# Layer 3 of a four-layer graph network: seven half-products with W1 in the place of eight, and one norm for both halves

## The chip, the cores and the metric

The kernel runs on one core of one Trainium2 chip. The metric is the device time of that core in microseconds (us): the time before is the median of three runs, 4798.12 us (4796.85 to 4800.23). The profile comes from one further, profiled execution.

## The reference

Sixteen graphs of 1024 nodes with 256 features pass through four layers, each of the form x = x + layer(relu(layernorm(x)), adj). All arithmetic is in float32. The change lies in layer 3 alone, which computes, per graph:

```
h   = relu(layernorm(x))                          # 1024 x 256
agg = epsilon * h + adjacency @ h                 # 1024 x 256
h   = agg @ W1 + b1                               # 1024 x 1024
h   = silu(h * rsqrt(mean(h*h, over its 1024 columns) + 1e-6) * rms_weight)
out = h @ W2 + b2                                 # 1024 x 256
x   = x + out
```

## The kernel before, in words

Layers 0 and 1, then layer 2 and then layer 3 follow one another; layer 3 starts near 3400 us of the span and takes the rest. It goes through the 16 graphs ("batches" b) one after the other. All of it works on transposed data: features lie on the 128 partitions, nodes along the free axis. N = 1024 nodes are cut into two halves of NH = 512[...]. D = 256 makes DC = 2 blocks of 128 features, H = 1024 makes HC = 8 blocks.

For each batch the functions inside `layer_3` do this:

- `load(b)` (L1105) issues the DMAs on SP's queue: x, the layer's other input hn, and the transposed adjacency in two halves `at[b][0]`, `at[b][1]`. Tiles come from pools with a fixed number of buffers per name; a load starts when a buffer of that name is free. hn lies in the pool `shared` under the name "hb", two buffers, which at the start hold x and hn of batch 0.
- `prepare(b)` (L1120) adds hn to x, takes mean and variance, and writes h = relu(layernorm(x)); VectorE does the adds and statistics, GpSimd the power -1/2 (L83) and the adds of epsilon on the diagonal of the adjacency (L1124), ScalarE the relus (L1143), and GpSimd at last adds b2 to x (L1146).
- `sums(b)` (L1148) is the product with the adjacency, in four parts (half of N, block of D), each eight matmuls of 512 columns into a bank "pa" (L1155), copied to the tile ag by ScalarE or VectorE (L1158, L1160).
- `inner(ag, n0, between)` (L1163) is the product with W1 for one half of N: for each of the 8 blocks k of H two matmuls (L1170) into a bank "ph" (two banks), then ScalarE squares it (L1173), VectorE copies it to hh with b1 (L1174), and GpSimd adds the squares up in ss (L1176). `between` names steps of the other half's norm to be put behind block k.
- `norm` (L1181) gives `mean` (four matmuls with a column of ones, L1188, and the power), `spread` (four transposes that put the result in a bank "pr", L1194) and `apply` (multiply by it on VectorE, L1199, and silu on ScalarE, L1200).
- `outer` (L1203) is the product with W2: for each of four tiles of 128 nodes eight matmuls of 256 columns into a bank "po" (L1208) and an add onto x (L1211). After the second half x goes out by a DMA on GpSimd's queue (L1245).

The order of the work is set by the loop at the end: inner of half 0; inner of half 1 with the mean and spread of half 0 in between; the four `apply` of half 0; part 0 of the next batch's `sums`; mean of half 1; part 1; spread of half 1; outer of half 0 with `apply` of half 1 between its tiles; part 2; `prepare(b + 2)`; part 3; outer of half 1. From this written order the framework makes each engine's queue: written order is the priority, and an instruction that would have to wait by its reckoning can be passed by a later one that is ready. `tc.issue_after(last)` keeps prepare's VectorE instructions behind the last add of the first `outer`. On the chip each engine runs its queue in order.

Of the kernel before, what the change touches and what calls it, by code (L numbers as in the profile page):

```python
# [9 lines left out]
F32 = mybir.dt.float32  # L10
AF = mybir.ActivationFunctionType
ALU = mybir.AluOpType
# [4 lines left out]
P = 128  # L17
B, N, D, H = 16, 1024, 256, 1024
NT = N // P
DC = D // P  # L20
HC = H // P
# [9 lines left out]
RMS_EPS = 1e-6  # L31
# [9 lines left out]
def gnn_stack(ctx: ExitStack, tc: tile.TileContext, a: dict, out: bass.AP):  # L41
    nc = tc.nc
# [3 lines left out]
    ident = const.tile([P, P], F32, name="ident")  # L46
    make_identity(nc, ident)
    ones = const.tile([P, P], F32, name="ones")
# [993 lines left out]

    def early_3(shared, pool, x, hn, at, h):


        eps = pool.tile([P, 1], F32, name="eps")
        nc.sync.dma_start(eps, bcast_row(a["epsilon"], 1))
        x[0] = shared.tile([P, NT, D], F32, name="hb")  # L1050
        nc.sync.dma_start(x[0], rows(x2_d[0]))
        at[0] = [shared.tile([P, NT, 512], F32, name="bxt")]
        for t in range(0, NT, 2):
            nc.sync.dma_start(at[0][0][:, t : t + 2], rows(a["adjT"][0])[:, t : t + 2, :512])
        hn[0] = shared.tile([P, NT, D], F32, name="hb")
        nc.sync.dma_start(hn[0][:, : NT - 2], rows(hn_d[0])[:, : NT - 2])
        nc.sync.dma_start(hn[0][:, NT - 2], hs_d[NT - 2][0][:P])
        eye = pool.tile([P, P], F32, name="eye")
        yield eye

        n = NT - 1
        nc.vector.tensor_scalar(eye, ident, eps, None, op0=ALU.mult)
        mv = pool.tile([P, n, 2], F32, name="mv")
        for t in range(n):
            nc.vector.tensor_add(x[0][:, t], x[0][:, t], hn[0][:, t])
            st = pool.tile([P, 6], F32, name="st", bufs=4)
            nc.vector.bn_stats(st, x[0][:, t])
            nc.vector.bn_aggr(mv[:, t], st)
            if t % 3 == 2:
                yield  # L1070
        rs = inv_sqrt(pool, mv[:, :, 1], LN_EPS, [P, n], "rs")
        for t in range(NT // 2):
            own = at[0][0][:, t, t * P : (t + 1) * P]
            nc.gpsimd.tensor_tensor(own, own, eye, ALU.add)
        yield
        h[0] = hn[0]
        shift = pool.tile([P, n], F32, name="shift")
        nc.vector.scalar_tensor_tensor(shift, mv[:, :, 0], -1.0, rs, op0=ALU.mult, op1=ALU.mult)
        for t in range(n):
            nc.scalar.activation(h[0][:, t], x[0][:, t], AF.Relu, bias=shift[:, t : t + 1], scale=rs[:, t : t + 1])  # L1080
        yield

    def layer_3(shared, x, hn, at, h, eye):
        with ExitStack() as st:
            wp = st.enter_context(tc.tile_pool(name="w3", bufs=1))
# [15 lines left out]
            nc.sync.dma_start(b2, bcast_row(a["b2"], D))  # L1101

            NH = 512

            def load(b):  # L1105
                if b:
# [11 lines left out]
                    at[b].append(half)  # L1118

            def prepare(b):  # L1120
                def diagonal(half):
                    for t in range(half * NT // 2, (half + 1) * NT // 2):
                        own = at[b][half][:, t, t * P % NH : t * P % NH + P]
                        nc.gpsimd.tensor_tensor(own, own, eye, ALU.add)  # L1124
                part = slice(0 if b else NT - 1, NT)
                if b:
                    diagonal(0)
                    h[b] = big.tile([P, NT, D], F32, name="h", bufs=2)
                tiles = range(NT)[part]
                mv = small.tile([P, NT, 2], F32, name="mv")  # L1130
                for t in tiles[::2]:
# [10 lines left out]
                for k, t in enumerate(tiles):  # L1142
                    nc.scalar.activation(h[b][:, t], x[b][:, t], AF.Relu, bias=shift[:, k : k + 1], scale=rs[:, k : k + 1])  # L1143
                diagonal(1)
                for t in range(NT):
                    nc.gpsimd.tensor_tensor(x[b][:, t], x[b][:, t], b2, ALU.add)  # L1146

            def sums(b):  # L1148

                ag = big.tile([P, DC, N], F32, name="ag")  # L1150

                def part(n0, c):
                    pa = psum.tile([P, NH], F32, name="pa")
                    for mt in range(NT):
                        nc.tensor.matmul(pa, h[b][:, mt, c * P : (c + 1) * P], at[b][n0 // NH][:, mt],  # L1155
                                         start=mt == 0, stop=mt == NT - 1)
                    if c == 0:
                        nc.scalar.copy(ag[:, c, n0 : n0 + NH], pa)  # L1158
                    else:
                        nc.vector.tensor_copy(ag[:, c, n0 : n0 + NH], pa)  # L1160
                return ag, [lambda n0=n0, c=c: part(n0, c) for n0 in range(0, N, NH) for c in range(DC)]

            def inner(ag, n0, between):  # L1163

                hh = big.tile([P, HC, NH], F32, name="hh")
                ss = small.tile([P, NH], F32, name="ss")
                for k in range(HC):
                    ph = psum.tile([P, NH], F32, name="ph")
                    for c in range(DC):
                        nc.tensor.matmul(ph, w1[:, c, k * P : (k + 1) * P], ag[:, c, n0 : n0 + NH],  # L1170
                                         start=c == 0, stop=c == DC - 1)
                    sq = ss if k == 0 else small.tile([P, NH], F32, name="sq")
                    nc.scalar.activation(sq, ph, AF.Square, bias=b1[:, k : k + 1])  # L1173
                    nc.vector.tensor_scalar(hh[:, k], ph, b1[:, k : k + 1], None, op0=ALU.add)  # L1174
                    if k:
                        nc.gpsimd.tensor_tensor(ss, ss, sq, ALU.add)  # L1176
                    if k in between:
                        between[k]()
                return hh, ss

            def norm(hh, ss):  # L1181

                got = {}

                def mean():
                    pq = psum.tile([P, NH // P], F32, name="pq", bufs=1)
                    for n in range(NH // P):
                        nc.tensor.matmul(pq[:, n : n + 1], ss[:, n * P : (n + 1) * P], ones[:, 0:1], start=True, stop=True)  # L1188
                    got["rms"] = inv_sqrt(small, pq, RMS_EPS, [P, NH // P], "rms", mul=1.0 / H)

                def spread():
                    pr = psum.tile([P, NH], F32, name="pr", bufs=1)
                    for n in range(NH // P):
                        nc.tensor.transpose(pr[:, n * P : (n + 1) * P], got["rms"][:, n : n + 1].to_broadcast([P, P]), ident)  # L1194
                    got["pr"] = pr

                def apply(quarter):
                    for k in (2 * quarter, 2 * quarter + 1):
                        nc.vector.tensor_mul(hh[:, k], hh[:, k], got["pr"])  # L1199
                        nc.scalar.activation(hh[:, k], hh[:, k], AF.Silu, scale=rw[:, k : k + 1])  # L1200
                return mean, spread, apply

            def outer(b, hh, n0, apply=None):  # L1203
                for k in range(NH // P):
                    t = n0 // P + k
                    po = psum.tile([P, D], F32, name="po")
                    for c in range(HC):
                        nc.tensor.matmul(po, hh[:, c, k * P : (k + 1) * P], w2[:, c], start=c == 0, stop=c == HC - 1)  # L1208
                    if apply:
                        apply(k)  # L1210
                    last = nc.vector.tensor_add(x[b][:, t], x[b][:, t], po)  # L1211
                return last.ins

            load(0)
            prepare(0)
            load(1)
            ag, parts = sums(0)
            for part in parts:
                part()
            prepare(1)  # L1220
            for b in range(B):
                if b + 2 < B:
                    load(b + 2)
                hh0, ss0 = inner(ag, 0, {})
                mean0, spread0, apply0 = norm(hh0, ss0)
                hh1, ss1 = inner(ag, NH, {1: mean0, 4: spread0})
                mean1, spread1, apply1 = norm(hh1, ss1)
                parts = [lambda: None] * 4
                if b + 1 < B:
                    ag, parts = sums(b + 1)  # L1230
                for k in range(4):
                    apply0(k)
                parts[0]()
                mean1()
                parts[1]()
                spread1()
                last = outer(b, hh0, 0, apply1)
                parts[2]()
                if b + 2 < B:

                    with tc.issue_after(last):
                        prepare(b + 2)
                parts[3]()
                outer(b, hh1, NH)
                nc.gpsimd.dma_start(rows(out[b]), x[b])  # L1245

    layers_0_1()
# [51 lines left out]
```

## Time and profile before

| what | value |
|---|---|
| median of three runs | 4798.12 us |
| the profiled execution's own time | 4804.16 us |
| its span, first to last instruction | 4802.5 us |
| mean granted TensorE clock | 0.979 |
| PE (matmul) busy | 4482.4 us, 93% |
| PEld (weight load) busy | 3004.1 us, 63% |
| DVE (VectorE) busy | 2250.0 us, 47% |
| POOL (GpSimd) busy | 1561.7 us, 33% |
| ACT (ScalarE) busy | 1238.4 us, 26% |

The groups of layer 3's window that matter for the change, each with its line, count, and the mean duration of one instruction:

| line, engine | what | count | mean ns |
|---|---|---|---|
| L1170 PE | matmul with W1, 512 columns | 1024 | 607 |
| L1208 PE | matmul with W2, 256 columns | 2048 | 379 |
| L1155 PE | matmul with the adjacency, 512 columns (two groups: 512 and 448 of the records) | 960 | 593 |
| L1173 ACT | square, from PSUM | 224 | 686 |
| L1174 DVE | copy with b1, from PSUM | 256 | 749 |
| L1176 POOL | add to ss | 224 | 1271 |
| L1199 DVE | multiply, one operand in PSUM | 256 | 680 |
| L1200 ACT | silu, from SBUF | 256 | 712 |
| L1158 ACT | copy from PSUM | 32 | 577 |
| L1160 DVE | copy from PSUM | 32 | 692 |
| L1133 DVE | add of two SBUF tiles, 512 columns | 60 | 692 |

How to read it: matmuls overlap in the pipeline, so that the mean duration of one is longer than the distance from one to the next. "Idle before, releaser" in a row is the time for which the engine stood still before an instruction, and what ended it. The chain is the work that ended last, followed back from its end. Where a row of the timeline has a count (x8), the time is that of the whole stretch.

### The profile page before, as it was taken

To read this page: it belongs to the slowest core of one execution; us is meant where nothing else is said; L and a number is where in the kernel's file an instruction comes from. 1 tells how busy PE (TensorE), PEld (TensorE's weight loads), DVE (VectorE), ACT (ScalarE), POOL (GpSimd) and SP (SyncE) were. 2 spreads that over 40 slices of the span, in tenths; PEclk is the share of its full clock that TensorE was granted. 3 is DMA by queue.
4 is the path that set the end of the run, shared out by engine and by line. 5 is a ranking of instruction groups with operands and counts; after the bars stand their busy time and mean duration, and the time that the engine had idled before them with its cause. 6 is when DMAs were issued, how large, how long until landed. Compare 5 with 4: busy or idle time off the path is not lost. (4 is left out here: it accounts for less than half of the span.)

```text
span 4802.5 us, 52444 instructions
## 1 busy us (share of the span) xinstructions
PE 4482.4 (93%) x18199; PEld 3004.1 (63%) x18199; DVE 2250.0 (47%) x6292; ACT 1238.4 (26%) x2629; POOL 1561.7 (33%) x1938
## 2 busy tenths in 40 slices
PE   8998899999997989999999999998899999999999
PEld 4444455555555777777777778777455565655656
DVE  6667845456543444444444444455333334334342
ACT  1111112212111222222332322233222323223232
POOL 3223233344323323232223232323333334333331
PEclk9999999999998999999999999999899999999999
DMA  4333235554546444544353445431422222222200
GB/s 152 115 105 105 80 80 185 198 179 155 183 130 197 127 150 126 157 133 152 111 158 117 141 142 176 129 124 39 136 88 97 79 88 79 88 97 79 79 27 18
DMA packets 530979, 576.63 MB, mean 120 GB/s; under 512 B 42544, under 2 KB 439472, under 8 KB 528304
## 3 DMA queue, kind: packets, MB, share of 16 engines
q1 hardware_dynamic: 499536, 460.27, 30.8%
q0 software_dynamic: 31040, 111.44, 6.7%
q8 instruction: 198, 3.24, 0.3%
q14 instruction: 205, 1.68, 0.1%
HBM read 469.65 MB, written 116.65 MB: 122 GB/s over the span
## 5 line engine op out<-in xcount | busy, mean ns | idle before, releaser
L295 PE MATMUL pa<-at,h 128*128 128x512 f32 x1088 | 502.2, 615 | 32.9 <-DVE ag L300 32.9
L1170 PE MATMUL ph<-ag,w 128*128 128x512 f32 x1024 | 467.3, 607 | 8.4 <-DVE hh L1174 8.3
L1208 PE MATMUL po<-w,hh 128*128 128x256 f32 x2048 | 447.7, 379 | 0.0
L623 PE MATMUL pf<-hb,ab 128*128 128x256 f32 x1568 | 419.1, 385 | 29.4 <-DVE bxt L773 16.2
L1208 PEld LDWEIGHTS po<-w,hh 128*128 128x128 f32 x2048 | 387.8, 190 | 59.3 <-issue 7.9
L295 PE MATMUL pa<-at,q 128*128 128x512 f32 x960 | 424.0, 595 | 0.0
L295 PEld LDWEIGHTS pa<-at,h 128*128 128x128 f32 x1088 | 211.6, 197 | 281.3 <-issue 235.5
L735 PE MATMUL pf<-hs,wx 128*128 128x256 f32 x1536 | 348.9, 381 | 18.7 <-POOL hs L726 16.1
L1170 PEld LDWEIGHTS ph<-ag,w 128*128 128x128 f32 x1024 | 179.8, 190 | 259.5 <-issue 146.5
L1176 POOL TENSOR_TENSOR ss<-ss,sq 128x512 f32<-128x512 f32 x224 | 284.6, 1271 | 149.9 <-ACT sq L1173 149.4
L735 PEld LDWEIGHTS pf<-hs,wx 128*128 128x128 f32 x1536 | 290.4, 191 | 61.4 <-POOL hs L726 17.9
L623 PEld LDWEIGHTS pf<-hb,ab 128*128 128x128 f32 x1568 | 277.7, 192 | 69.3 <-DVE bxt L773 23.5
L295 PEld LDWEIGHTS pa<-at,q 128*128 128x128 f32 x960 | 178.2, 190 | 215.9 <-issue 212.6
L1174 DVE TENSOR_SCALAR hh<-ph,b 128x512 f32<-128x512 f32 x256 | 191.6, 749 | 219.1 <-ACT sq L1173 171.0
L770 PE MATMUL pf<-bd,h 128*128 128x384 f32 (+5 forms) x768 | 213.9, 372 | 49.1 <-DVE bxt L773 26.5
L1022 POOL DMA_INDIRECT hs_d<-h,table x128 | 129.6, 1012 | 368.7 <-ACT gates L743 184.5
L1155 PE MATMUL pa<-at,h 128*128 128x512 f32 x512 | 225.8, 593 | 0.0
L83 POOL TENSOR_TENSOR rs<-rs_v,mhalf 128x8 f32<-128x8 f32 (+1 forms) x65 | 106.9, 1644 | 346.0 <-DVE rs_v L79 332.5
L1173 ACT ACTIVATE sq<-ph,b 128x512 f32<-128x512 f32 x224 | 153.6, 686 | 223.2 <-PE ph L1170 218.1
L773 DVE TENSOR_TENSOR bxt<-bxt,pf 128x384 f32<-128x384 f32 (+5 forms) x384 | 141.3, 384 | 144.3 <-PE pf L770 141.8
L1200 ACT ACTIVATE hh<-hh,rw 128x512 f32<-128x512 f32 x256 | 168.5, 712 | 142.4 <-DVE hh L1199 140.4
L1155 PE MATMUL pa<-bxt,h 128*128 128x512 f32 x448 | 197.4, 593 | 0.0
(261 smaller groups left out, 7271.7 us busy)
## 6 DMA issues: line engine op xcount, KB each, us to landing
at<-in_adjT SPq DMA_DIRECT2D x64, 1024.0 KB, 7.2
ab<-in_adj SPq DMA_DIRECT2D x128, 512.0 KB, 4.1
bxt<-in_adjT SPq DMA_DIRECT2D x64, 512.0 KB, 5.8
at<-in_adjT SPq DMA_DIRECT2D x64, 512.0 KB, 5.8
ad<-in_adj SPq DMA_DIRECT2D x128, 128.0 KB, 5.7
x_d<-x POOLq DMA_DIRECT2D x16, 1024.0 KB, 5.4
he_d<-h POOLq DMA_DIRECT2D x16, 1024.0 KB, 9.2
heT_d<-hT POOLq DMA_DIRECT2D x16, 1024.0 KB, 4.2
```

Source lines behind the costliest of these rows:

```text
L295: nc.tensor.matmul(pa, h[:, mt, c * P : (c + 1) * P], at[n0 // 512][:, mt], start=mt == 0, stop=mt == NT - 1)
L623: nc.tensor.matmul(pb, ab[:, jts[k]], hb[:, jts[k]], start=k == 0, stop=k == len(jts) - 1)
L735: nc.tensor.matmul(pg[:, e], wx[:, c, q * D + e * P : q * D + (e + 1) * P], self.hs[:, c], start=c == 0, stop=c == DC - 1)
L770: nc.tensor.matmul(pf, h[:, g, c * P : (c + 1) * P], bd[:, g, b4 : b4 + 4, S : S + far], start=True, stop=True)
L773: return lambda: nc.vector.tensor_add(to, to, pf)
L1155: nc.tensor.matmul(pa, h[b][:, mt, c * P : (c + 1) * P], at[b][n0 // NH][:, mt], start=mt == 0, stop=mt == NT - 1)
L1170: nc.tensor.matmul(ph, w1[:, c, k * P : (k + 1) * P], ag[:, c, n0 : n0 + NH], start=c == 0, stop=c == DC - 1)
L1173: nc.scalar.activation(sq, ph, AF.Square, bias=b1[:, k : k + 1])
L1174: nc.vector.tensor_scalar(hh[:, k], ph, b1[:, k : k + 1], None, op0=ALU.add)
L1176: nc.gpsimd.tensor_tensor(ss, ss, sq, ALU.add)
L1200: nc.scalar.activation(hh[:, k], hh[:, k], AF.Silu, scale=rw[:, k : k + 1])
L1208: nc.tensor.matmul(po, hh[:, c, k * P : (k + 1) * P], w2[:, c], start=c == 0, stop=c == HC - 1)
```

## The change

In layer 3 the product of agg with W1 is seen as a 2 x 2 block product: D in two halves (c), H in two halves (p), N in two halves. The eight half-products become seven, after Strassen (in Winograd's form). Three combinations of W1's quarters (`ws`) and one that takes the place of a quarter (a21) are made once per kernel by four adds on GpSimd. Per batch four combinations of the sums (`tt`) are made by VectorE. `inner` handles both halves of N at once: for each of four k it does seven products, each one matmul of 512 columns; ScalarE copies the first to SBUF (p1), VectorE adds the next two up (u2, u3), and four results are formed by VectorE with b1 (`result`), then squared by ScalarE from SBUF and added up by GpSimd. The seventh product is accumulated onto the bank of the fourth after VectorE has read that.

With it change the buffers and the order. `mean` and `spread` treat both halves at once and stand after part 0 and part 1 of the next batch's sums; parts 2 and 3 follow, then the first `outer`, then `prepare(b + 2)`, then the second `outer`. ag has one buffer (before: two). The banks "pa" and "ph" become five banks "ph"; "pq", "pr" and "po" become three banks "po". h of a batch is written over hn in its buffer, and x of batch 0 moves to a buffer of its own when b2 is added. All four parts of the sums are copied by ScalarE.

```diff
@@ layer_3, once
+            HH = HC // 2
+            ws = wp.tile([P, 3, HH * P], F32, name="ws")
+            a11, a12, a21, a22 = (w1[:, c, p * HH * P : (p + 1) * HH * P] for p in range(2) for c in range(2))
+            nc.gpsimd.tensor_tensor(ws[:, 0], a21, a22, ALU.add)
+            nc.gpsimd.tensor_tensor(ws[:, 1], ws[:, 0], a11, ALU.subtract)
+            nc.gpsimd.tensor_tensor(a21, a11, a21, ALU.subtract)
+            nc.gpsimd.tensor_tensor(ws[:, 2], a12, ws[:, 1], ALU.subtract)
@@ prepare
-                    h[b] = big.tile([P, NT, D], F32, name="h", bufs=2)
+                    h[b] = hn[b]
...
+                to = x[b] if b else big.tile([P, NT, D], F32, name="x", bufs=3)
                 for t in range(NT):
-                    nc.gpsimd.tensor_tensor(x[b][:, t], x[b][:, t], b2, ALU.add)
+                    nc.gpsimd.tensor_tensor(to[:, t], x[b][:, t], b2, ALU.add)
+                x[b] = to
@@ sums
-                ag = big.tile([P, DC, N], F32, name="ag")
+                ag = big.tile([P, DC, N], F32, name="ag", bufs=1)
+                tt = big.tile([P, 4, NH], F32, name="tt", bufs=1)
+                b21 = []
...
-                    pa = psum.tile([P, NH], F32, name="pa")
+                    pa = psum.tile([P, NH], F32, name="ph", bufs=5)
...
-                    if c == 0:
-                        nc.scalar.copy(ag[:, c, n0 : n0 + NH], pa)
-                    else:
-                        nc.vector.tensor_copy(ag[:, c, n0 : n0 + NH], pa)
+                    nc.scalar.copy(ag[:, c, n0 : n0 + NH], pa)
+                    if (n0, c) == (0, 1):
+                        b21.append(pa)
+                    if (n0, c) == (NH, 0):
+                        nc.vector.tensor_sub(tt[:, 0], pa, ag[:, 0, :NH])
+                    if (n0, c) == (NH, 1):
+                        nc.vector.tensor_sub(tt[:, 1], pa, tt[:, 0])
+                        nc.vector.tensor_sub(tt[:, 2], pa, ag[:, 0, NH:])
+                        nc.vector.tensor_sub(tt[:, 3], b21[0], tt[:, 1])
@@ inner, for both halves of N
-                for k in range(HC):
-                    ph = psum.tile([P, NH], F32, name="ph")
-                    for c in range(DC):
-                        nc.tensor.matmul(ph, w1[:, c, k * P : (k + 1) * P], ag[:, c, n0 : n0 + NH],
-                                         start=c == 0, stop=c == DC - 1)
-                    sq = ss if k == 0 else small.tile([P, NH], F32, name="sq")
-                    nc.scalar.activation(sq, ph, AF.Square, bias=b1[:, k : k + 1])
-                    nc.vector.tensor_scalar(hh[:, k], ph, b1[:, k : k + 1], None, op0=ALU.add)
-                    if k:
-                        nc.gpsimd.tensor_tensor(ss, ss, sq, ALU.add)
-                    if k in between:
-                        between[k]()
+                hh = [big.tile([P, HC, NH], F32, name=f"hh{q}", bufs=1) for q in range(2)]
+                ss = [small.tile([P, NH], F32, name=f"ss{q}", bufs=1) for q in range(2)]
+                begun = [False, False]
+
+                def product(lhsT, rhs, onto=None):
+                    ph = onto if onto is not None else psum.tile([P, NH], F32, name="ph", bufs=5)
+                    nc.tensor.matmul(ph, lhsT, rhs, start=onto is None, stop=True, skip_group_check=onto is not None)
+                    return ph
+
+                def result(k, q, ph, u):
+                    nc.vector.scalar_tensor_tensor(hh[q][:, k], ph, b1[:, k : k + 1], u, op0=ALU.add, op1=ALU.add)
+                    sq = small.tile([P, NH], F32, name="sq") if begun[q] else ss[q]
+                    nc.scalar.activation(sq, hh[q][:, k], AF.Square)
+                    if begun[q]:
+                        nc.gpsimd.tensor_tensor(ss[q], ss[q], sq, ALU.add)
+                    begun[q] = True
+
+                for k in range(HH):
+                    mine = slice(k * P, (k + 1) * P)
+                    p1, u2, u3 = (small.tile([P, NH], F32, name=name) for name in ("p1", "u2", "u3"))
+                    ph = product(a11[:, mine], ag[:, 0, :NH])
+                    nc.scalar.copy(p1, ph)
+                    ph = product(ws[:, 1, mine], tt[:, 1])
+                    nc.vector.tensor_add(u2, ph, p1)
+                    ph = product(a21[:, mine], tt[:, 2])
+                    nc.vector.tensor_add(u3, ph, u2)
+                    p5 = product(ws[:, 0, mine], tt[:, 0])
+                    result(HH + k, 1, p5, u3)
+                    result(HH + k, 0, product(a22[:, mine], tt[:, 3]), u3)
+                    result(k, 0, product(a12[:, mine], ag[:, 1, :NH]), p1)
+                    result(k, 1, product(ws[:, 2, mine], ag[:, 1, NH:], p5), u2)
@@ norm: mean and spread for both halves, apply inside spread
+                    pq = psum.tile([P, N // P], F32, name="po", bufs=3)
...
+                    for q in range(2):
+                        pr = psum.tile([P, NH], F32, name="po", bufs=3)
...
+                        for k in range(HC):
+                            nc.vector.tensor_mul(hh[q][:, k], hh[q][:, k], pr)
+                            nc.scalar.activation(hh[q][:, k], hh[q][:, k], AF.Silu, scale=rw[:, k : k + 1])
@@ the loop over batches
-                hh0, ss0 = inner(ag, 0, {})
-                mean0, spread0, apply0 = norm(hh0, ss0)
-                hh1, ss1 = inner(ag, NH, {1: mean0, 4: spread0})
-                mean1, spread1, apply1 = norm(hh1, ss1)
+                hh, ss = inner(*ags)
+                mean, spread = norm(hh, ss)
...
-                for k in range(4):
-                    apply0(k)
                 parts[0]()
-                mean1()
+                mean()
                 parts[1]()
-                spread1()
-                last = outer(b, hh0, 0, apply1)
+                spread()
                 parts[2]()
+                parts[3]()
+                last = outer(b, hh, 0)
                 if b + 2 < B:

                     with tc.issue_after(last):
                         prepare(b + 2)
-                parts[3]()
-                outer(b, hh1, NH)
+                outer(b, hh, 1)
```

## The prediction

> **What bounds the kernel now.** I read the table of engines first (PE busy 93% of the span), then a window over one batch of layer 3 in mid-run, then the chain in that window, then the weight loads, which show stalls that a pipelined matmul row hides, and last the first batch. The window is 86.10 us, from one batch's first product with W1 to the next batch's:
>
> ```profile
> core 0: us, PE busy (x) PEld busy (x) DVE busy (x) ACT busy (x) POOL busy (x), PEclk, DMA share, GB/s
> 4476.70:4494.56 17.86, 17.86 (x41) 6.94 (x40) 7.18 (x10) 6.18 (x9) 9.79 (x8) 1.00 0.35 118
> 4494.56:4507.23 12.67, 12.67 (x39) 6.07 (x38) 8.13 (x14) 7.17 (x11) 8.64 (x7) 1.00 0.00 1
> 4507.23:4521.44 14.21, 14.21 (x44) 6.98 (x43) 2.24 (x5) 3.21 (x5) 2.30 (x2) 1.00 0.00 0
> 4521.44:4562.80 41.36, 41.36 (x163) 30.40 (x161) 14.76 (x39) 9.64 (x17) 10.69 (x17) 1.00 0.29 102
> ```
>
> PE is busy throughout at full clock, and no other engine reaches 70% of the first two rows, the stage of `inner`. The chain in that window is PE alone:
>
> ```profile
> by line: PE ph L1170 35.5%; PE po L1208 34.5%; PE pa L1155 27.6%; PE pq L1188 1.6%; PE pr L1194 0.9%
> 4476.86 17.87 PE ph L1170 x40
> 4494.73 0.79 PE pq L1188 x8
> 4495.51 5.43 PE ph L1170 x12
> 4501.38 3.44 PE ph L1170 x8
> 4505.68 1.72 PE ph L1170 x4
> ```
>
> Every float32 matmul of the source is two records (1024 on L1170 for 512 calls). The eight in 3.44 us give 0.429 us a record, 0.858 us a call; the group's mean of 607 ns overlaps its neighbours and is not the price. At 0.429 the 64 records of L1170 need 27.4 us; they took 17.87+5.43+3.44+1.72 = 28.46. The missing 1.0 us shows in the weight loads, where each second k waits for VectorE to empty one of two PSUM banks (0.68 us against the ordinary 0.24 "issue"):
>
> ```profile
> 4479.27 0.19 PEld L1170 LDWEIGHTS ph<-ag,w 128*128 128x128 f32 x1 [0.24 <-issue]
> 4480.14 0.30 PEld L1170 LDWEIGHTS ph<-ag,w 128*128 128x128 f32 x2 [0.68 <-DVE hh L1174]
> ```
>
> So in this layer a matmul removed is time removed, as long as nothing slower takes the stage.
>
> **Removed.** For the output blocks k and k+4 and both halves of N, eight calls become seven: 28 calls of the same shape per batch in place of 32, 4 x 0.858 = 3.4 us. The two-bank stall goes too (five banks now): 1.0 us. The means and transposes keep their counts (8 and 8 calls a batch; 2.5 us before, 2.5 after), `sums` and `outer` keep theirs (27.5 and 27.6 us). A clean batch is then 24.0 + 2.5 + 27.5 + 27.6 = 81.7 us, 4.4 us less.
>
> **Added in the stage, per k of four, beside 7 x 0.858 = 6.0 us of PE:**
> - VectorE: two adds of PSUM and SBUF (nearest row L1199, 680 ns) and four scalar_tensor_tensor. No row has that one at 512 columns: at 256, L397 takes 481 ns against 420 for an add (L1211), so 680+61, about 0.74; L1174 at 512 columns takes 749. I take 0.75. Sum 2 x 0.69 + 4 x 0.75 = 4.4 us, under 6.0.
> - ScalarE: a copy (L1158, 577 ns) and four squares, now from SBUF (L1200 reads SBUF: 712; L1173 reads PSUM: 686): 0.59 + 4 x 0.7 = 3.4 us.
> - GpSimd: four adds into ss as before, 1.27 us each: 5.1 us (14 adds, 17.8 us a batch, under 24.0).
>
> Whether GpSimd stretches when VectorE works harder: the two rows disagree by kind of operand. In the first batch an add of two SBUF tiles beside an ss add slowed both (the two L1133 took 2.36 us where they take 1.29, the ss add 1.55); an L1199 (one operand in PSUM) beside ss adds shows 675 to 689 throughout. All six new operations have one operand in PSUM, so L1199 is near: no stretch. The upper bound is 1.55.
>
> One rule speaks against leaving this add where it is. The row is L1176's 1271 ns against 692 for L1133 on VectorE. The Trainium skill, page GPSIMD Engine Reference, section 4.1 Engine selection, sends elementwise adds of two inputs to VectorE since GpSimd is about twice as slow. By the rule the 14 adds would be 9.7 us on VectorE, whose stage would be 17.5 + 9.7 = 27.2 us against PE's 24.0, and a batch would gain 28.46 - 27.2, just over 1 us. By the rows, 17.8 us on GpSimd lie under 24.0. I go by the rows.
>
> **The new wait.** Product 7 accumulates onto product 4's bank, so it waits for VectorE's first result. Behind it in PE's queue stand the next k's products; who waits for them is the copy p1. From the start of a k: product 1 readable at 0.86 + 0.2 (in the window, first matmul 4476.86, first square 4478.61: two calls plus 0.04 to 0.2), p1 to 1.65, product 2 readable 1.92, u2 to 2.6, product 3 at 2.77, u3 to 3.5, product 4 at 3.63, result to 4.4. Product 7's weights load at 4.9: slack 0.5 us, no stall.
>
> Over several k there is a loop: ScalarE may square the fourth result before it copies p1 of the next k, and a square needs one of two sq tiles, freed by GpSimd. If it does, the loop from one first result to the next is square 0.72, two GpSimd adds 2.6, square 0.74, copy 0.59, u2 0.72, u3 0.69, result 0.75 = 6.8 us, over 6.0. It has no hold in k = 0, whose first two squares go to ss directly; worked forward it costs PE 0.4 us in k = 2 and 0.8 in k = 3, 1.2 us a batch. If the copy goes first, the loop loses a square and an add, and at 4.8 to 5.5 us is under 6.0: 0. The trace before shows ScalarE's later-written silus slipped between squares that wait, so I take 0 and keep 1.2.
>
> **The joint norm.** From the last product: result 0.95, square 0.7, add 1.3, about 3 us, 4.5 with a backlog. The first part of `sums`, 8 calls, 6.9 us, stands between and hides it. The power (1.02 for four columns, 1.65 for eight) and two handoffs lie under the second part's 6.9. After the transposes VectorE's 16 multiplies (0.64 each in a row, 10.3) and ScalarE's 16 silus (0.66, 10.6) run about 12 us under parts three and four, 13.7 us; the first half is ready after 6.5. The four subtractions and ScalarE's copies of the sums (2.8 us, 2.3) follow, and `outer` gives them 27 us. All at 0. Without this cover each exposed us costs 15.
>
> **Prepare moves behind the fourth part.** Before, from its first VectorE add at 4449.69 to shift at 4457.38 is 7.7 us, the relus end about 4462.1, GpSimd's b2 adds at 4464.1: 14.4 us. It began 27.5 us ahead of the next `inner`; now 13.8. All it issues counts: VectorE's 22 operations stand ahead of `outer`'s adds of the second half (three PSUM banks give PE 10.3 us, need 7.7: 0), the relus ahead of the next p1, the b2 and diagonal adds ahead of the output's DMA and of the first ss add, which comes 5 us into `inner`. 0, at most 1 us a batch. Loads on SP's queue: h in hn's buffer frees it only after the sums, which still leaves half a batch or more.
>
> **First and last batch, and the weights.** Batch 0 lasted 96.8 us (3432.51 to 3529.32), 10.7 over a clean one: hn of batch 1 waited for a buffer until 3432.74, and its prepare fell into `inner`:
>
> ```profile
> 3438.53 2.36 DVE L1133 TENSOR_TENSOR x<-x,hb 128x512 f32<-128x512 f32 x2 [0.92 <-DMA hb<-hn_d]
> 3446.08 5.46 PE L1170 MATMUL ph<-ag,w 128*128 128x512 f32 x8 [6.43 <-DVE hh L1174]
> ```
>
> Now x of batch 0 leaves its buffer when the b2 adds end (3421.7), so hn loads some 10 us earlier; its relus and b2 adds still reach into `inner`. I take half, 5 us back (0 to 10). The last batch has no sums to hide the norm: result, square, add, means, power, transposes, multiply, silu expose about 8 us, and the first tile goes at the silus' pace, 5.6 for 3.45: its chain is some 61.5 to 64 us for 60.0 now. I take +3, so no saving there. The four weight sums on GpSimd (5.1 us) can delay the power at 3411.15 if W1 lands first: +1 (0 to 5).
>
> Sum against the profiled execution (4802.5 span, 4804.16 its own time): 14 batches x -4.4 = -62; batch 0 -4.4 - 5; last +3; weights +1: -67.4, so 4736.8. It ran 6.0 over the median of the runs: **4731**.
>
> **Rivals.**
> - ScalarE takes the square before the copy: 15 x 1.2 = 18 more, 4749. For it: that is the order written. Against: a square that waits lets others past.
> - The norm is not covered (means wait for ss by 2 us or more a batch): 4731 + 15 x 2 to 3, about 4770. Against: 6.9 us of cover for 4.5.
> - Slower: GpSimd becomes the bound in that loop, at ss. It decides when the loss reaches the 4.4 us gained: about 2.2 loop turns a batch bite, so a loop of 8.0 us, adds of 1.9 us. At 2.2 us the loop is 8.7, 5.9 us a batch are lost and 1.5 net, and with the first and last batch the kernel stands near 4820. Against: 1.55 is the slowest ss add in the trace.
> - The matmuls removed were not on the path: 4798. Against: the chain.
>
> **Chances.** The forecast 0.52 (its own range 4718 to 4742), the loop in the written order 0.28, the norm exposed 0.09, no change 0.04, slower 0.07. About 0.2% (9.6 us) is what a measurement here can tell from no change. Faster 0.89, same 0.04, slower 0.07. Range: low, batch 0 gives all 10 back and weights and tail cost nothing, 4722, less 4 for overlap of the means; high, the loop's case with batch 0 giving nothing, the weights at 5 and prepare at 0.7 a batch: 4769.
>
> **What would show it.** A batch of 81.7 us, 56 records of the products in 24.0, their weight loads idle 0.24 throughout; waits of PE on the second result line near zero. A p1 copy that starts after the fourth square, with squares waiting on ss, shows the loop; PE waiting on ss at the means, the norm. The forecast is wrong if ss adds pass 1.5 us, or if VectorE's new operations pass 0.9 us.

## The result, and the profile after

The changed kernel takes 4758.98 us (median of four runs, 4754.82 to 4763.29) where the kernel before takes 4799.17 beside it (4796.85 to 4805.13): a ratio of 0.9914, 95% interval 0.9897 to 0.9932. The forecast was 4731 in a range of 4718 to 4769; the time lies in the range, but 28 us behind the forecast, and nearer to the rival of the written order, 4749. It lies in the range because that was drawn wide enough for this rival; the forecast itself had put the rival's cost at nothing.

The profiled execution has a span of 4753.1 us, 49.4 less than before. Not all of that is the change's: layer 3's first matmul starts at 3392.10 where it started at 3401.66, and over the runs of this study it started between 3386 and 3402 us, in no order that follows the edits. So I compare layer 3 alone, from its first matmul to the end of the span: 1400.8 us before, 1361.0 after, 39.8 less.

One batch after, in two windows (columns as before): the seven products, then the rest up to the next batch's first product. They sum to 83.08 us, 86.10 before.

```profile
core 0: us, PE busy (x) PEld busy (x) DVE busy (x) ACT busy (x) POOL busy (x), PEclk, DMA share, GB/s
4428.55:4453.88 25.33, 24.57 (x58) 10.48 (x57) 16.42 (x24) 10.47 (x18) 14.62 (x14) 1.00 0.26 83
4453.88:4511.63 57.75, 57.75 (x217) 39.09 (x216) 21.94 (x52) 17.81 (x31) 16.06 (x21) 1.00 0.26 91
```

The second row is what was forecast (2.5 + 27.5 + 27.6 = 57.6 us): the joint norm, the subtractions and the moved prepare cost PE nothing. The first is not: 25.3 us for 24.0, and PE is idle for 0.8 of it. The chain over this batch (in the window of both rows), which was PE alone before, now leaves PE for a fifth of the time:

```profile
by line: PE po L1251 33.5%; PE ph L1176 33.2%; PE ph L1197 8.6%; POOL ss L1205 6.1%; ACT sq L1203 3.8%; DVE hh L1201 3.7%; DVE u L1216 2.5%; DVE u L1214 2.5%; PE po L1231 2.0%; ACT p L1212 1.7%; issue 1.3%; PE po L1239 1.1%; DVEq L1216 0.1%
```

Its pieces in order of time (start, us, what), from one first result of a k to the next:

```profile
4438.34 0.76 DVE hh L1201
...
4439.18 0.64 ACT sq L1203
...
4439.95 2.52 POOL ss L1205 x2
...
4442.50 0.63 ACT sq L1203
4443.13 0.48 ACT p L1212
...
4443.64 0.70 DVE u L1214
...
4444.43 0.70 DVE u L1216
...
4445.23 0.76 DVE hh L1201
```

This is the loop of the prediction, operation by operation: result, square, two adds on GpSimd, the square that waited for a buffer, the copy behind it, u2, u3, the next result. From 4438.34 to 4445.23 it takes 6.89 us; 6.8 was worked out. The weight loads show where it meets PE, at product 7 of k = 2 and k = 3 (idle 0.98 and 1.44 us for the ordinary 0.24):

```profile
4446.03 0.30 PEld L1197 LDWEIGHTS ph<-ag,ws 128*128 128x128 f32 x2 [0.98 <-DVE hh L1201]
4452.91 0.30 PEld L1197 LDWEIGHTS ph<-ag,ws 128*128 128x128 f32 x2 [1.44 <-DVE hh L1201]
```

Product 7 of k = 2 starts 0.3 us late and that of k = 3 another 0.8; with 0.1 us for each restart that is 1.3 us a batch.

The first batch: PE waits longer for h than before (3.18 us, was 1.31: the row alone is before, the two are after), and batch 0 then stops at its second product; batch 0 lasts from 3424.81 to 3514.58, 89.8 us for 96.8 before.

```profile
3412.66 20.01 PE L1155 MATMUL pa<-bxt,hb 128*128 128x512 f32 x46 [1.31 <-ACT hb L1143]
```

```profile
3404.97 20.01 PE L1176 MATMUL ph<-bxt,hb 128*128 128x512 f32 x46 [3.18 <-ACT hb L1160]
3430.47 2.05 PE L1197 MATMUL ph<-tt,ws 128*128 128x512 f32 x2 [4.63 <-DVE tt L1184]
```

The last batch: the norm stands bare between the products and outer. From its first product (4677.78) to the last matmul's end (4745.63) it takes 67.9 us, 60.0 before. Before, the means of half 1 stood between matmuls of `outer` and waited less than 1 us (the row alone is before, the three are after):

```profile
4767.52 1.05 PE L1188 MATMUL pq<-ones,ss 128*128 128x1 f32 x8 [0.96 <-POOL ss L1176]
```

```profile
4706.83 3.45 PE L1231 MATMUL po<-ones,ss 128*128 128x1 f32 x16 [3.58 <-POOL ss L1205]
4712.27 1.97 PE L1239 MATMUL po<-ident,rms 128*128 128x128 f32 x8 [2.00 <-POOL rms L83]
4714.92 30.71 PE L1251 MATMUL po<-w,hh 128*128 128x256 f32 x128 [0.68 <-ACT hh L1243]
```

The sixteen records of the means take 3.45 us where they take 1.84 in the other batches: the granted clock in the window from 4703 to 4715 us is 0.67. The Trainium skill (TensorE: Matmul & The Clock Gate, Part 1) puts the drop to half the clock at about 3.4 us of idling; the 3.58 us here agree with it, shorter gaps in other runs do not (last section).

### The profile page after: what moved, and what is told of

Same layout as the page of the kernel before. It is cut to its first block, busy times and chain, and to the rows that moved or that the text cites. A ratio compares the mean times of both kernels' runs of the same rounds, so it can differ in the third digit from the quotient of the medians.

```text
span 4753.1 us, 52478 instructions
## 1 busy us (share of the span) xinstructions
PE 4421.1 (93%) x18071; PEld 2991.8 (63%) x18071; DVE 2344.1 (49%) x6436; ACT 1271.5 (27%) x2725; POOL 1554.1 (33%) x1926
## 5 line engine op out<-in xcount | busy, mean ns | idle before, releaser
L295 PE MATMUL pa<-at,h 128*128 128x512 f32 x1088 | 497.0, 610 | 32.9 <-DVE ag L300 32.9
L1205 POOL TENSOR_TENSOR ss<-ss,sq 128x512 f32<-128x512 f32 x224 | 279.9, 1269 | 165.5 <-ACT sq L1203 161.7
L770 PE MATMUL pf<-bd,h 128*128 128x384 f32 (+5 forms) x768 | 213.9, 372 | 49.5 <-DVE bxt L773 26.5
L1176 PE MATMUL ph<-bxt,hb 128*128 128x512 f32 x512 | 226.0, 597 | 4.0 <-ACT hb L1160 3.2
L1176 PE MATMUL ph<-at,hb 128*128 128x512 f32 x512 | 224.3, 593 | 0.0
L1242 DVE TENSOR_TENSOR hh<-hh,po 128x512 f32<-128x512 f32 x256 | 154.4, 679 | 111.6 <-PE po L1239 111.6
L740 DVE TENSOR_TENSOR gates<-pf,bias 128x512 f32<-128x512 f32 x128 | 88.3, 691 | 220.1 <-PE pf L735 205.4
L1203 ACT ACTIVATE sq<-hh 128x512 f32<-128x512 f32 x224 | 141.1, 630 | 194.8 <-DVE hh L1201 128.4
L770 PEld LDWEIGHTS pf<-bd,h 128*128 128x128 f32 x768 | 132.4, 192 | 94.4 <-DVE bxt L773 41.8
L829 ACT ACTIVATE r<-pr 128x256 f32<-128x256 f32 (+3 forms) x230 | 68.1, 348 | 405.8 <-PE pr L788 382.1
```

The costliest lines, as they stand in the source:

```text
L295: nc.tensor.matmul(pa, h[:, mt, c * P : (c + 1) * P], at[n0 // 512][:, mt], start=mt == 0, stop=mt == NT - 1)
L770: nc.tensor.matmul(pf, h[:, g, c * P : (c + 1) * P], bd[:, g, b4 : b4 + 4, S : S + far], start=True, stop=True)
L1203: nc.scalar.activation(sq, hh[q][:, k], AF.Square)
L1205: nc.gpsimd.tensor_tensor(ss[q], ss[q], sq, ALU.add)
L1242: nc.vector.tensor_mul(hh[q][:, k], hh[q][:, k], pr)
```

## The experiments

The theory is that the 1.3 us a batch are the loop through the two buffers of squares and GpSimd's adds. The rival is that VectorE's six operations a k and the copy are by themselves too slow a chain for PE. "Layer 3" is from its first matmul to the end of the span, a batch from one first product to the next, both from the profiled execution. Beside these kernels the one before took between 4795.76 and 4800.57 us; the ratio holds against the runs beside each kernel.

| kernel | median us | ratio to before (95%) | layer 3 us | batch us |
|---|---|---|---|---|
| before | | | 1400.8 | 86.1 |
| changed | 4758.98 | 0.9914 (0.9897 to 0.9932) | 1361.0 | 83.1 |
| four buffers of squares | 4736.34 | 0.9881 (0.9866 to 0.9897) | 1340.1 | 81.8 |
| copy first | 4740.46 | 0.9881 (0.9866 to 0.9896) | 1340.3 | 81.8 |
| eight products | 4784.92 | 0.9979 (0.9969 to 0.9989) | 1391.5 | 85.2 |
| adds on VectorE | 4736.87 | 0.9880 (0.9865 to 0.9895) | 1343.7 | 82.1 |
| adds twice | 4954.01 (one run) | | 1562.4 | 95.5 |
| start | 4727.27 (one run) | | 1336.4 | 81.8 |
| start and end | 4735.62 | 0.9868 (0.9851 to 0.9885) | 1337.4 | 81.8 |
| all | 4724.43 | 0.9852 (0.9833 to 0.9871) | 1328.3 | 81.8 |
| changed, again | 4754.45 | 0.9911 (0.9895 to 0.9928) | 1358.2 | 83.1 |

**Four buffers of squares.**

```diff
-                    sq = small.tile([P, NH], F32, name="sq") if begun[q] else ss[q]
+                    sq = small.tile([P, NH], F32, name="sq", bufs=4) if begun[q] else ss[q]
```

> The changed kernel with four buffers for the squares in the place of two; every engine's queue is in the same order as in the changed kernel. Theory (the loop through the squares' two buffers and GpSimd's adds sets when product 7 may start): the fourth square no longer waits for GpSimd, so the copy p1 comes 0.7 to 1.3 us sooner in k = 2 and 3; the product stage falls from 25.3 to 24.0 us, a batch from 83.06 to 81.8, the kernel by 18 to 20 us against the changed kernel, to about 4740. Rival (VectorE's six operations and ScalarE's copy are themselves too slow a chain for PE): the stage stays at 25.3 us and the time near 4759.

A batch takes 81.79 us, its product stage 24.03. ScalarE's row in that stage shows the wait gone: the third and fourth square follow their results, and the copy follows them, in the same order of the queue as in the changed kernel.

```profile
4091.96 1.35 ACT L1203 ACTIVATE sq<-hh 128x512 f32<-128x512 f32 x2 [2.47 <-DVE hh L1201]
4093.54 0.63 ACT L1203 ACTIVATE sq<-hh 128x512 f32<-128x512 f32 x1 [0.23 <-DVE hh L1201]
4094.39 0.63 ACT L1203 ACTIVATE sq<-hh 128x512 f32<-128x512 f32 x1 [0.23 <-DVE hh L1201]
4094.93 0.57 ACT L1212 COPY p<-ph 128x512 f32<-128x512 f32 x1
```

PE has no wait on a result any more. The rival falls: VectorE's and ScalarE's operations are all still there.

**Copy first.** The next k's first product and its copy (made by `first`) are written ahead of the third and fourth result; two buffers stay. In part:

```diff
+                p1 = first(0)
                 for k in range(HH):
...
                     result(HH + k, 0, product(a22[:, mine], tt[:, 3]), u3)
-                    result(k, 0, product(a12[:, mine], ag[:, 1, :NH]), p1)
+                    now = p1
+                    if k + 1 < HH:
+                        p1 = first(k + 1)
+                    result(k, 0, product(a12[:, mine], ag[:, 1, :NH]), now)
```

> The changed kernel with two buffers for the squares, but the first product of the next k and its copy p1 are written ahead of the third and fourth result of this k, so that ScalarE copies before it squares them. Theory (the copy stands behind a square that waits for GpSimd): the copy is out of the loop, the stage falls to about 24.0 us and the kernel to about 4740, as with four buffers. Rival (VectorE's chain is too slow): stage 25.3 us, near 4759, since the same operations run on the same engines.

81.79 us a batch again. The edit also puts product 7 one call later, which by itself gives it 0.86 us more slack. But in k = 0 to 3 the first results now start 6.0 us apart where they were up to 6.89 apart, so the loop is gone and not only covered:

```profile
4178.46 1.61 DVE L1201 SCALAR_TENSOR_TENSOR hh<-ph,b,u 128x512 f32<-128x512 f32 x2 [0.16 <-PE ph L1197]
...
4184.47 1.61 DVE L1201 SCALAR_TENSOR_TENSOR hh<-ph,b,u 128x512 f32<-128x512 f32 x2 [0.16 <-PE ph L1197]
...
4190.47 1.61 DVE L1201 SCALAR_TENSOR_TENSOR hh<-ph,b,u 128x512 f32<-128x512 f32 x2 [0.16 <-PE ph L1197]
...
4196.48 1.61 DVE L1201 SCALAR_TENSOR_TENSOR hh<-ph,b,u 128x512 f32<-128x512 f32 x2 [0.16 <-PE ph L1197]
```

So the loop needs both: the square that waits, and the copy behind it in ScalarE's queue. Either removed, it is gone.

**Adds twice.**

```diff
                     if begun[q]:
+                        spare = small.tile([P, NH], F32, name="spare", bufs=1)
+                        nc.gpsimd.tensor_tensor(spare, ss[q], sq, ALU.add)
                         nc.gpsimd.tensor_tensor(ss[q], ss[q], sq, ALU.add)
```

> The changed kernel with every GpSimd add of a square made twice, the first time into a tile that nobody reads (the output stays as it is). Theory (loop through GpSimd): the loop from one first result to the next was 6.9 us and gets two adds more, 9.4 us; GpSimd itself then needs 8 x 1.27 = 10.2 us per k, so k = 1, 2 and 3 come every 9.4 to 10.2 us, the stage goes from 25.3 to some 31 to 33 us, and the means wait for ss besides, 3 to 6 us a batch: a batch of 92 to 96 us, the kernel near 4930, slower than the kernel before: the slower rival of the prediction at an add of 2.5 us. Rival (VectorE's chain): no more than the overhang at the end of the stage, 5 us a batch at most.

A batch takes 95.5 us and the kernel 4954 (4930 expected). GpSimd now sets the pace: its 28 adds of a batch follow each other every 1.3 us, from 4393.32 to 4430.04, 36.7 us for PE's 24.0. Over layer 3 PE waits 57 us for the copy p1, 35 for the first result and 35 for ss at the means. The slower rival of the prediction was a true threat. Its place, GpSimd in the loop and at ss, is right; adds of 2 us or more did not occur by themselves. Its price was too low: by the prediction's count (2.2 turns of the loop a batch) 2.54 us for each square would cost about 7 us a batch, and they cost 13.7 (95.5 for 81.8).

**Eight products.** Each k and half has two accumulating matmuls again; weight sums and `tt` are left out; the rest of the change stays. In part:

```diff
-                    p5 = product(ws[:, 0, mine], tt[:, 0])
-                    result(HH + k, 1, p5, u3)
...
+                    for c in range(DC):
+                        nc.tensor.matmul(ph, w1[:, c, k * P : (k + 1) * P], ag[:, c, q * NH : (q + 1) * NH],
+                                         start=c == 0, stop=c == DC - 1)
+                    nc.vector.tensor_scalar(hh[q][:, k], ph, b1[:, k : k + 1], None, op0=ALU.add)
```

> The changed kernel with the products undone alone: eight calls of two accumulating matmuls per k, no weight sums, no combinations of the sums; the joint norm, the five banks, the moved prepare and the buffers stay. Theory: no second-bank stall and no loop, PE at its rate, stage 27.4 us, batch 85.2 us for 86.1 before: 0.9 x 14 = 13 us gained, batch 0 gives some 7 back, the uncovered norm of the last batch costs 6: about 4785, so the joint norm and the banks alone are worth some 14 us and the seven products the rest. Rival (most of the gain is the joint norm and the reordering): within 5 us of the changed kernel's 4759.

4784.92 us and 85.2 us a batch, as expected. The joint norm, the banks and the new order are worth 9.3 us of layer 3 (about 14 x 0.9 and 4.8 in batch 0, less 7.1 in the last batch, 0.5 at the start and 0.4 behind the last matmul); the seven products are worth the other 30.5 (1391.5 to 1361.0), and 51 with the loop broken.

**Adds on VectorE.** This is the rule that the prediction weighed and turned down.

```diff
-                        nc.gpsimd.tensor_tensor(ss[q], ss[q], sq, ALU.add)
+                        nc.vector.tensor_add(ss[q], ss[q], sq)
```

> The changed kernel with the 14 adds of the squares on VectorE in the place of GpSimd. Theory: VectorE then needs 6 x 0.7 + 4 x 0.69 = 6.9 to 7.1 us per k, over PE's 6.0; the stage is VectorE's, some 26.5 to 27.5 us, a batch about 84.5, the kernel about 4775, with 3 us of that given back in the last batch. Rival (the GpSimd adds are what is slow, so any faster engine helps): stage near 24.0, kernel near 4740.

The expectation is wrong: 4736.87 us, a batch of 82.06. VectorE's part was sized rightly: from u2 of k = 0 at 4251.34 to the last add's end at 4277.84 it works 26.5 us. But PE does not wait for it. At the end of a stage VectorE and PE stand as follows:

```profile
4275.64 0.74 DVE L1201 SCALAR_TENSOR_TENSOR hh<-ph,b,u 128x512 f32<-128x512 f32 x1
4276.31 0.68 DVE L1205 TENSOR_TENSOR ss<-ss,sq 128x512 f32<-128x512 f32 x1
4277.15 0.69 DVE L1205 TENSOR_TENSOR ss<-ss,sq 128x512 f32<-128x512 f32 x1 [0.16 <-ACT sq L1203]
```

```profile
4273.67 1.02 PE L1197 MATMUL ph<-ag,ws 128*128 128x512 f32 x2
4274.52 6.17 PE L1176 MATMUL ph<-at,hb 128*128 128x512 f32 x14
4280.53 1.84 PE L1231 MATMUL po<-ones,ss 128*128 128x1 f32 x16
```

PE is through its products by 4274.5 and goes on with the next batch's sums; the first thing that needs ss are the means at 4280.5, by which time VectorE is 2.7 us ahead of them. VectorE's overhang of some 3 us lies under the 6.9 us that hide GpSimd's. What of its delay reaches product 7 is 0.17 us in k = 2 and, in k = 3, a pair of records of the sums that stands there in its place.

**Start.** Four buffers; the weight sums written behind `prepare(0)`; prepare's relus of batch 1 behind the last copy of batch 0's sums. In part:

```diff
             prepare(0)
+            nc.gpsimd.tensor_tensor(ws[:, 0], a21, a22, ALU.add)
...
             for part in parts:
-                part()
-            prepare(1)
+                copied = part()
+            with tc.issue_after(copied):
+                prepare(1)
```

> Four buffers for the squares, the four weight sums written behind prepare of batch 0, and the relus of batch 1's prepare queued on ScalarE behind the last copy of batch 0's sums. Theory: the power of batch 0 no longer stands behind the weight sums, PE's wait for h falls from 3.2 to 1.3 us; the copy that the combinations of the sums wait for comes first, the 4.6 us wait of batch 0's second product and some 2 us of lower clock after it go; layer 3 is 6 to 8 us shorter than with four buffers alone, its batches stay at 81.8 us. Rival (the wait is for data or for VectorE): the second product still waits 4 us.

Half of it came. The second product waits 1.3 us for 4.2, and batch 0 takes 83.9 us for 88.7 with four buffers alone. But PE's wait for h is 2.9 us as there: W1 lands first, and the framework put the weight sums ahead of the power all the same. Layer 3 is 3.7 us shorter, not 6 to 8: batch 0 gives 4.8 and the last batch takes 1.2 more (66.0 us for 64.8, its means at the lower clock).

**Start and end.** The same, and the last batch with eight products, half after half: `halves` puts the mean of half 0 behind k = 2 of half 1 and its spread behind k = 4. The combination that takes the place of a21 gets a tile of its own, so that W1 stays whole. In part:

```diff
+                if b + 1 == B:
+                    halves(b, ags[0])
+                    nc.gpsimd.dma_start(rows(out[b]), x[b])
+                    break
```

> As the run before this one, and the last batch alone with eight products, half after half, the first half's norm inside the second half's products as in the kernel before (a21's replacement gets a buffer of its own). Theory: the 8 us by which the last batch became longer are the norm that nothing hides; with it hidden the last batch takes 60 us from its first product to its last matmul in the place of 66.5, and the kernel comes to about 4724, 1.5% under before. Rival (the last batch is long because of the lower clock or the output's DMA): it stays near 66 us.

A miss: the last batch takes 68.2 us. The norm stood bare once more, at another place:

```profile
4687.96 1.87 PE L1259 MATMUL po<-ones,ss 128*128 128x1 f32 x8 [5.50 <-POOL ss L1280]
```

The eight multiplies of half 0 (4.9 us on VectorE, from 4677.58) had slipped in front of the last three results of half 1, so that ss came 5.5 us late, and no matmul of outer was written between.

**All.** The multiplies of half 0 are written behind half 1's products, one tile of outer ahead of half 1's mean and one between its mean and spread; the weight sums are queued behind the power. In part, against the run before:

```diff
+                apply(0)
+                outer(b, hh, 0, (0,))
                 mean(1)
+                outer(b, hh, 0, (1,))
                 spread(1)
-                outer(b, hh, 0)
+                apply(1)
+                outer(b, hh, 0, (2, 3))
                 outer(b, hh, 1)
...
+            with tc.issue_after(powers[-1]):
+                nc.gpsimd.tensor_tensor(ws[:, 0], a21, a22, ALU.add)
```

> Four buffers for the squares; the weight sums queued on GpSimd behind the power of batch 0; the relus of batch 1 behind the last copy of batch 0's sums; the last batch with eight products, half after half, now with the first half's multiplies written behind the second half's products and the tiles of the first outer between the second half's mean and spread. Theory (the last batch is long because nothing hides the norm; in the run before, the first half's multiplies had slipped in front of the second half's last results and the norm stood bare all the same): PE waits for ss under 1.5 us, the last batch takes some 60 to 61 us from its first product to its last matmul where it took 68; PE's wait for h at the start falls from 2.9 to about 1.3 us; layer 3 is some 8 us shorter than with the last but one set of edits, the kernel near 4724. Rival (the last batch is long for another reason, as the lower clock): 66 us or more.

The last batch takes 58.9 us, PE's wait for ss is 0.7:

```profile
4686.21 2.75 PE L1249 MATMUL po<-w,hh 128*128 128x256 f32 x12
4689.68 1.05 PE L1261 MATMUL po<-ones,ss 128*128 128x1 f32 x8 [0.71 <-POOL ss L1285]
4690.59 4.56 PE L1249 MATMUL po<-w,hh 128*128 128x256 f32 x20
```

So the last batch's length was the bare norm, and the lower clock came with its waits: over this last batch (4657.41 to 4716.31) the granted clock is 1.00. The wait for h is 2.3 us, not 1.3, for a reason that the section on the hardware gives. What the start gains over the run before (31.8 us from the first matmul to the first product, for 34.0) batch 0 loses (85.2 us for 82.8): counted from the first matmul, hn of batch 1 loads no sooner (20.5 us, 20.0 in the run before), so that `shift` of batch 1 (3429.70) falls behind the last copy of the sums (3427.39), and the combinations stand behind `shift` in VectorE's queue. This is the fastest version, 0.9852 of the time before: it has the seven products without the loop, and a last batch that hides its norm.

**Changed, again.**

> The changed kernel itself, timed beside the run before it on one chip: about 4759 us, a batch of 83.06 us, layer 3 of 1361 us from its first matmul to the end. It gives the spread of what stands in front of layer 3, which the change does not touch.

4754.45 us, layer 3 in 1358.2, 2.8 us less than in the other profile: batch 0 is 2.3 us shorter (its second product waited 2.35 us here and 4.63 there), the last batch 1.6 shorter, the start 1.3 longer; the full batches are the same.

## Why the forecast was right in kind and 28 us short

The sum of the prediction beside layer 3's parts, before and after:

| term | forecast us | measured us | from |
|---|---|---|---|
| 14 full batches | -62 | -42.5 | 1205.7 to 1163.2 |
| batch 0 | -9.4 | -7.0 | 96.8 to 89.8 |
| last batch | +3 | +7.8 | 60.0 to 67.9 |
| weights, start | +1 | +1.9 | 30.9 to 32.7 |
| sum | -67.4 | -39.8 | 1400.8 to 1361.0 |

- **Removed.** Right. With the loop broken a batch is 81.79 us; 81.7 was worked out (86.10 less 4.4; the four terms written there add up to 81.6). Calls of 0.858 us, the two-bank stall (86.1 to 85.2 with eight products), 57.6 us for the rest: each holds.
- **Added operations.** Right: 692 ns for u2 and u3, 746 to 747 for the results, 572 for the copy, 630 for the square, less than the 0.7 taken. GpSimd's add stayed at 1269 ns beside them, so the row of L1199 was the right one.
- **The new wait.** Right within a k: no product 7 waits in k = 0 or 1.
- **The loop over several k.** This is the step that failed: "so I take 0 and keep 1.2". The loop, its 6.8 us and its 1.2 us a batch were right (6.89 and 1.3), the choice between the two orders was wrong: 14 x 1.3 = 18 us of the 28. The evidence for the choice was weak: silus that pass a waiting square say that something later may pass, not that this copy would. In the trace the copy stands behind the fourth square in every k, and where that waits it waits with it (ScalarE idle 0.60 us before the squares at 4442.50 and 4449.38).
- **The joint norm.** Right in the full batches, 57.75 us for 57.6.
- **Prepare behind part four.** Right at 0: GpSimd ends its b2 adds about 1 us after the stage's start, and the first ss add comes 5.9 us after that.
- **Last batch.** The mechanism was right, the size not: 7.8 for 3. The loop's 1.3 us count here too; the norm exposed 11.8 us for 8 (from the last product's end near 4703.1 to 4714.92, with the means at the lower clock), and outer at the silus' pace and the lower clock took 3 us more than in a full batch.
- **Batch 0.** Near what was taken, and for the reason given: 4.0 us given back for 5 (6.7 over a full batch, 10.7 before), and hn's DMA starts 10 us earlier, counted from layer 3's first matmul. The relus still reached into `inner`, as said; what was not said is where that costs: half of them (from 3427.05) stand ahead of the copy (3429.03) that the combinations wait for.
- **Weights.** +1.9 for +1: the four sums stand ahead of the power.
- **The rule turned down.** Turning it down was wrong: "a batch would gain 28.46 - 27.2, just over 1 us" put the stage at its longest engine, and with the adds on VectorE a batch gains 4.0 (86.10 to 82.06), where the change as it stands gains 3.0. An engine that only produces for a later stage may run over by as much as the work between covers. In GpSimd's favour stands only that with four buffers its adds cost no more (81.79).

## What to carry to other kernels

Where a matmul waits for an engine that waits for another, sum the loop from one such wait to the next over all queues that it crosses, buffers and in-order neighbours included, and hold that against PE's time for the same stretch: VectorE, ScalarE and GpSimd at 41 to 65% of the stage said nothing here, and the loop of 6.89 us against 6.0 took nearly a third of a batch's gain. If the sum is over and only an assumed order of a queue saves it, count the loss, or give the buffer that opens the loop: here two more tiles of 512 columns were worth 18 to 21 us of layer 3. Work that was hidden by the next item has no cover in the last one; give that one its own order, and look in the trace whether the order came out as written.

## What the runs showed of the hardware that was not expected

A VectorE instruction of one column was held by a whole GpSimd add. In the last version the weight sum starts on GpSimd just ahead of `shift`, whose two tensors are in SBUF, and `shift` takes 1.22 us where it took 0.16 before; they end together (the first row is before).

```profile
3411.77 0.16 DVE L1141 SCALAR_TENSOR_TENSOR shift<-mv,rs 128x1 f32<-128x1 f32 x1 [0.84 <-POOL rs L83]
```

```profile
3405.38 1.22 DVE L1155 SCALAR_TENSOR_TENSOR shift<-mv,rs 128x1 f32<-128x1 f32 x1 [0.84 <-POOL rs L85]
```

```profile
3405.33 1.25 POOL L1302 TENSOR_TENSOR ws<-w 128x512 f32<-128x512 f32 x1
```

That is the 1 us by which the wait for h stayed too long. The Trainium skill (SBUF — State Buffer, SBUF: two separate sides) has it as an exclusive lock on a pair of ports between the two engines, taken by a VectorE operation with two SBUF inputs against a GpSimd one that reads SBUF; the rows agree, while the results and adds with one operand in PSUM went beside GpSimd's adds at their usual 0.69 and 0.75 us.

The length of a gap did not settle whether the clock fell. With the adds on VectorE the means of the last batch waited 2.65 us and their sixteen records took 3.57 us, at a mean granted clock of 0.50 (4687.37 to 4691.00). With four buffers they waited 3.11 us and the first eight still went at full speed (granted clock 1.00 from 4681.16 to 4682.40); the clock fell only behind them. So the page's 3.4 us is no bound on which to plan a gap, and where the two differ the measurement decides:

```profile
4687.37 3.57 PE L1231 MATMUL po<-ones,ss 128*128 128x1 f32 x16 [2.65 <-DVE ss L1205]
```

```profile
4681.16 1.05 PE L1231 MATMUL po<-ones,ss 128*128 128x1 f32 x8 [3.11 <-POOL ss L1205]
```
